# Two cross-attention layers on one core: the softmax factors of layer 0 applied by GpSimd to the exponentials, one step ahead of their turn

## The chip, the core and the metric

The kernel runs on one core of a Trainium2 chip. A core has five engines that run side by side, each with its own queue of instructions taken in order: TensorE (PE, matrix products), VectorE (DVE), ScalarE (ACT), GpSimd (POOL) and SyncE (SP), which here issues DMA transfers. They wait for each other by semaphores. TensorE writes to PSUM, eight banks of 128 x 512 fp32 values; SBUF holds everything else. The metric is device time in microseconds (us) for the whole program, from its start to its end; smaller is better. All data are fp32.

## What is computed

There are four batches of 1024 rows `x` (512 wide) and 1024 context rows (384 wide), and two attention layers one after the other. Cut to what matters:

```python
# layer 0: 16 heads of 64
h = layernorm(x, gamma, beta)
Q, K, V = (h @ Wq), (context @ Wk), (context @ Wv)        # by heads
attn = softmax(Q K^T, axis=-1) * 64 ** -0.5
x = x + (attn V) @ Wo + bo
# layer 1: 16 heads of 32
xn = x * rsqrt(mean(x * x) + eps) * norm_w
q, k, v = xn @ wq, split(context @ wkv)
q, k = normalized(rotated(q)), normalized(rotated(k))
x = x + (softmax(q k^T * sqrt(32)) v) @ wout
```

Note that the scale of layer 0 stands after the softmax: each row of exponentials is divided by its sum `l` and multiplied by 1/8.

## The kernel before

The work of a batch runs in two stages, layer 0 and then layer 1; the change concerns layer 0 and the passage from one to the other.

**Steps of layer 0.** Heads go in pairs: `NPAIR` = 8 pairs `p`, two heads `j` of 64 features each, side by side in the 128 partitions. For each pair there are `NT` = 8 steps `i`, one per tile of 128 query rows. So a batch has 64 steps and the program 256. One step (`Attention0.step`, L381) does this:

- `scores` (L367): four fp32 matrix products write the scores of 128 queries against 1024 keys for both heads into two PSUM tiles, `s`. There are just two such tiles, so the scores of the next step wait until the exponentials of this one have read theirs.
- For each head VectorE takes the negated maximum of a row (L395), and ScalarE writes the exponential to `e` in SBUF and its row sum to `l` (L396).
- VectorE turns `e` in 32 x 32 blocks (L401). Two steps (`BQ` = 2) make a block; after the odd step SP issues sixteen transfers of 128 KB each (L407) that put the 32 x 32 pieces where a whole transposition wants them, in `eT`.
- VectorE takes 1/l (L408).

**Products and factors.** A block of `eT` stands in the queue `self.blocks` until `product` (L443) multiplies it with the values `v`: 32 matmuls of 256 columns. Since `eT` has the keys in the partitions, the result `av` has features in the partitions and queries along the free axis, and the factors 1/l, which belong to queries, have to be spread along the features and transposed as well. `factors` (L418) lets GpSimd spread them, times 1/8, into `rb`; `factors_turned` (L431) has TensorE transpose `rb` into PSUM (`rT`, two 128 x 128 transposes, L440) and ScalarE copy it into `vals` (L441); the product ends with a VectorE multiply of `av` and these factors into `vals` (L456). All this is done in even steps, right after the scores, once two blocks are waiting: the block of steps 2 and 3 is multiplied in step 6.

**Filling.** All the other work of TensorE, the projections of later pairs, the output products `po` of earlier pairs and the first projections of layer 1, is cut into units with a cost in us. `Units.fill(us)` issues units until that cost is spent. The main loop (L798 to L809) divides what is left by the steps left, takes off the cost of a product (`AV` = 3.9) in steps that have one, and hands the rest to `step`. Before the change 1.8 us of a step's filling stand between the exponentials and the turns, the rest at the end. Filling units can bring VectorE additions (L301), ScalarE evacuations (L130), GpSimd work and DMA issues. The work of `rotate` (L494, the rotation of layer 1's q and k on all engines) can be put behind the turns by `post` and `flush`.

**Order on the queues.** Everything is issued by hand in program order; each engine takes its own instructions in that order. A transfer that waits on SP holds the loads and stores issued after it.

**Buffers.** `e` and `eT` (tag `big`) have two buffers each, `qk` (keys and queries of a pair, and of layer 1) four. PSUM banks `f0` to `f3` go round for all products but the scores.

**Change of layer** (L820 to L835). After the last step two blocks wait. Their products are put into the units: the first at once, the second after four output tiles, the statistics of layer 1's norm, and one projection.

## Time and profile before

| What | us |
|---|---|
| median of three runs | 2974.82 (2970.41 to 2974.82) |
| the profiled execution | 2969.33 |
| its span, first to last instruction | 2967.1 |
| one batch of layer 0, first scores of a batch to its last, batch 0 | 442 (25.5 to 467.3) |
| the four batches' stretches 60:480, 784:1214, 1518:1950, 2253:2685 together | 1714.0, of which PE 1699.0, DVE 1328.7, ACT 708.7, POOL 158.9 busy |
| pairs 6 and 7 of batch 0, 386:472 | 86.0, of which PE 84.8, DVE 76.1, POOL 19.4 busy |
| TensorE clock granted | 0.999 of full |

A row of the groups reads: line, engine, operation, tiles out<-in with shapes, xcount, then busy us in total and mean ns of one, then the idle time of the engine just before them and which work ended it. A row of the timeline reads: start and duration in us, engine, line, operation, tiles, how many were merged, and in brackets the idle time before and what ended it. "SPq" rows are the issuing of transfers, not the transfers themselves; a transfer lands later. A matmul's duration includes its way through the array, so two matmuls one after the other overlap, and what one costs is seen from start to start. The counted matmuls are twice those in the code where the array is split in two column halves.

Three more groups of the page that are not shown below: the factors' copy on ScalarE (L441) has 128 rows of 373 ns, VectorE's multiply with them (L456) 128 of 408 ns, its reciprocals (L408) 256 of 124 ns.

### The profile page before, as it was taken

How to read it: one execution, taken by the hardware profiler on the slowest of the kernel's cores; microseconds unless marked ns; L12 is line 12 of the kernel's file. 1: busy time of each engine (PE TensorE's matmuls, PEld its weight loads, DVE VectorE, ACT ScalarE, POOL GpSimd, SP SyncE). 2: the span in 40 equal slices, each digit the busy share in tenths (PEclk: the TensorE clock that was granted, in tenths of full speed). 3: DMA queues.
4: the chain of work that ended last, by engine and by line, in shares of the span. 5: the costliest groups of instructions: out<-in, count | busy, mean ns of one | idle time of the engine just before them, and what ended most of it. 6: DMA issues, size and time to landing. Idle time of an engine off the chain costs nothing.

```text
span 2967.1 us, 66793 instructions
## 1 busy us (share of the span) xinstructions
PE 2905.4 (98%) x27880; PEld 1454.7 (49%) x27880; DVE 2230.9 (75%) x2824; ACT 1430.4 (48%) x2265; POOL 417.2 (14%) x392
## 2 busy tenths in 40 slices
PE   8999999999999999999999999999999999999998
PEld 4544445555544444555544444455455444445544
DVE  4777795877777779587777777958767777785777
ACT  3444443666544444466644444446664443444664
POOL 0010022420000002232000000224100000023310
PEclk9999999999999999999999999999999999999999
DMA  5787674010388867301048777730105978772000
GB/s 146 173 198 181 158 178 111 21 35 25 80 205 192 186 159 179 91 22 35 25 100 214 182 182 171 165 79 22 35 25 120 211 177 186 166 171 62 2 2 30
DMA packets 177549, 348.88 MB, mean 118 GB/s; under 512 B 37600, under 2 KB 93152, under 8 KB 177248
## 3 DMA queue, kind: packets, MB, share of 16 engines
q1 hardware_dynamic: 175056, 343.43, 48.9%
q8 instruction: 220, 3.60, 0.5%
q10 hardware_dynamic: 2192, 1.19, 0.1%
q14 instruction: 81, 0.66, 0.1%
HBM read 67.64 MB, written 8.39 MB: 26 GB/s over the span
## 4 chain that ended last, share of the span: by engine, by line
PE 85%; DVE 7%; DMA 2%; ACT 2%; SPq 1%; issue 1%; POOL 1%; DVEq 0%; ACTq 0%
PE s L372 16%; PE av L449 14%; PE po L158 11%; PE pv L158 8%; PE s L597 7%; PE pqT L158 7%; PE av L636 6%; PE pkT L158 5%; PE q_p L158 3%; PE av L647 2%; PE k_p L158 2%; DVE both L613 2%; PE rT L440 1%; DVE both L617 1%; SPq L407 1%
## 5 line engine op out<-in xcount | busy, mean ns | idle before, releaser
L396 ACT ACTIVATE e<-s,m 128x1024 f32<-128x1024 f32 x512 | 566.1, 1110 | 666.3 <-DVE m L395 625.8
L395 DVE TENSOR_REDUCE m<-s 128x1 f32<-128x1024 f32 x512 | 602.7, 1219 | 314.0 <-PE s L372 314.0
L607 ACT ACTIVATE e<-s 128x1024 f32<-128x1024 f32 x512 | 496.7, 1022 | 312.4 <-PE s L597 297.3
L401 DVE STREAM_TRANSPOSE e<-e 128x1024 f32<-128x1024 f32 x512 | 606.7, 1223 | 47.6 <-ACT e L396 44.7
L372 PE MATMUL s<-qk 64*128 64x512 f32 x2048 | 521.3, 615 | 5.4 <-ACT e L396 4.7
L449 PE MATMUL av<-eT,v 128*64 128x256 f32 x4096 | 465.2, 380 | 7.3 <-DMA eT<-e 3.7
L613 DVE TENSOR_TENSOR both<-e 128x512 f32<-128x512 f32 x512 | 342.1, 700 | 125.0 <-ACT e L607 89.8
L449 PEld LDWEIGHTS av<-eT,v 128*64 128x64 f32 x4096 | 295.1, 137 | 186.2 <-issue 48.4
L372 PEld LDWEIGHTS s<-qk 64*128 64x128 f32 x2048 | 182.4, 186 | 269.2 <-issue 193.3
L597 PE MATMUL s<-q,k 32*128 32x256 f32 x4096 | 305.1, 401 | 5.8 <-ACT q L524 2.7
L597 PEld LDWEIGHTS s<-q,k 32*128 32x128 f32 x4096 | 191.2, 184 | 149.2 <-ACT e L607 72.0
L158 PE MATMUL po<-wo,vals 128*64 128x512 f32 x1024 | 239.7, 599 | 3.0 <-ACT v L130 3.0
L158 PE MATMUL pqT<-hT,w 128*64 128x512 f32 (+1 forms) x1216 | 241.4, 598 | 0.7 <-ACT hT L255 0.7
L441 ACT COPY vals<-rT 128x256 f32<-128x256 f32 x128 | 47.8, 373 | 323.7 <-PE rT L440 323.7
L301 DVE TENSOR_TENSOR x<-x,po 128x512 f32<-128x512 f32 x200 | 134.0, 678 | 83.0 <-PE po L158 82.7
L158 PEld LDWEIGHTS pv<-w,cT 128*64 128x64 f32 (+1 forms) x3648 | 168.5, 128 | 34.3 <-issue 31.2
L158 PE MATMUL pv<-w,cT 128*64 128x128 f32 (+1 forms) x3648 | 183.4, 274 | 0.0
L158 PE MATMUL pkT<-cT,w 128*64 128x512 f32 (+1 forms) x912 | 182.0, 601 | 0.9 <-ACT cT L130 0.9
L617 DVE TENSOR_TENSOR both<-both 128x1024 f32<-128x1024 f32 x128 | 159.7, 1248 | 4.4
L636 PE MATMUL av<-e,v 128*32 128x256 f32 x2048 | 137.1, 385 | 0.0
L636 PE MATMUL av<-e,rest 128*32 128x256 f32 x2048 | 137.0, 385 | 0.0
L158 PE MATMUL q_p<-wq,hT 128*32 128x256 f32 (+1 forms) x1920 | 131.2, 380 | 0.0
(461 smaller groups left out, 2482.0 us busy)
## 6 DMA issues: line engine op xcount, KB each, us to landing
eT<-e SPq DMA_DIRECT2D x2048, 128.0 KB, 2.4
xr<-in_x_dram SPq DMA_DIRECT2D x32, 256.0 KB, 4.1
x<-in_x_dram SPq DMA_DIRECT2D x32, 256.0 KB, 3.7
wo<-in_Wo_dram SPq DMA_DIRECT2D x16, 512.0 KB, 4.2
out_dram<-x SPq DMA_DIRECT2D x32, 256.0 KB, 2.6
w<-in_Wq_dram SPq DMA_DIRECT2D x31, 256.0 KB, 4.0
c<-in_ctx_dram SPq DMA_DIRECT2D x32, 192.0 KB, 3.8
wkv<-in_wkv_dram SPq DMA_DIRECT2D x16, 384.0 KB, 3.2
```

The costliest lines, as they stand in the source:

```text
L158: nc.tensor.matmul(o[rr], lhsT[:, rr], rhs, start=start, stop=stop)
L301: nc.vector.tensor_add(xt[t], xt[t], pp[0])
L372: nc.tensor.matmul(sc[j][:, kb * 512 : (kb + 1) * 512], pr["qT"][r[j], i * P : (i + 1) * P], pr["kT"][r[j], kb * 512 : (kb + 1) * 512], st ...
L395: nc.vector.tensor_reduce(m[:, j : j + 1], sc[j], AX.X, ALU.max, negate=True)
L396: nc.scalar.activation(e[j], sc[j].rearrange("p (g s) -> p g s", g=4), AF.Exp, bias=m[:, j : j + 1], accum_out=l[:, j : j + 1])
L401: nc.vector.transpose(e[j], e[j])
L449: nc.tensor.matmul(av[r[j], :W].rearrange("p (t a i) -> p t a i", t=BQ, a=4), pr["v"][:, k, r[j]], eT[:, j, :, :, k * 32 : (k + 1) * 32], ...
L597: nc.tensor.matmul(sc[j // 2][:, j % 2, c, :], kT[rr, g, k * P : (k + 1) * P], qT[rr, g, qb * WQ : (qb + 1) * WQ], start=True, stop=True,)
L607: nc.scalar.activation(e, sc[u], AF.Exp, scale=float(np.sqrt(np.float32(HD1))))
L613: nc.vector.tensor_add(self.both[:, kk, 2 * u : 2 * u + 2, :], es[u][:, :, 0, :], es[u][:, :, 1, :])
L617: nc.vector.tensor_add(self.both[:, 0], self.both[:, 0], self.both[:, kk])
L636: nc.tensor.matmul(self.av[rr, 0, :], v[g][:, 2 * kk + c, rr], es[j // 2][:, j % 2, c, :], start=first and c == 0, stop=end and c == 1,)
```

## The change

GpSimd multiplies each head's exponentials by 1/l and by 1/8, in place, before they are turned. VectorE turns them not in their own step but in the next one, between the two reciprocals of that step. In even steps the exponentials go to a tile of their own, `raw`, and the turn carries them into the block's tile `e`; in odd steps they go to `e` at once. The sixteen transfers of a block are issued in the following even step, after the turns. The product, now without factors, is evacuated by ScalarE (`evac`) and is issued in odd steps right after the exponentials' and turns' instructions, ahead of all filling, which now stands at the end of the step in one piece. The spread, transposed and copied factors are gone, and so are `post` and `flush`: `rotate` is issued where it arises.

`qk` has three buffers instead of four; the keys of layer 1 are allocated at pair 6 by a unit, its queries after layer 0, and the second half's queries lie in the buffer of `raw`. The output products of earlier pairs are added to the units at step 4 instead of 3. At the change of layer `end` turns the last step's exponentials and issues the last block's transfers; the two products then stand after four output tiles, the norm's statistics and a projection, and after the norm, its transposes and three more units' groups.

```diff
         def step(self, p, i, pr, us):
             n = f"{self.b}_{p}_{i}"
             sc = self.scores(p, i, pr)
-            if i % BQ == 0 and len(self.blocks) == 2:
-                self.factors_turned()
...
+            li = sb.tile([P, 2], F32, tag="li", bufs=3, name=f"li_{n}")
+            if i % BQ:
                 self.e = sb.tile([P, 4, BQ * 2, S // 4], F32, tag="e", bufs=2, name=f"e0_{n}")
-                self.li = sb.tile([P, BQ, 2], F32, tag="li", bufs=4, name=f"li_{n}")
-            e = [self.e[:, :, i % BQ * 2 + j, :] for j in range(2)]
+                e = [self.e[:, :, 2 + j, :] for j in range(2)]
+            else:
+                if self.raw is None:
+                    self.raw = sb.tile([P, 2, S], F32, tag="raw", bufs=1, name=f"raw_{self.b}")
+                e = [self.raw[:, j].rearrange("p (g s) -> p g s", g=4) for j in range(2)]
             for j in range(2):
                 nc.vector.tensor_reduce(m[:, j : j + 1], sc[j], AX.X, ALU.max, negate=True)
                 nc.scalar.activation(e[j], sc[j].rearrange("p (g s) -> p g s", g=4), AF.Exp, bias=m[:, j : j + 1], accum_out=l[:, j : j + 1])
-            holds["posts"] = True
-            self.u.fill(min(us, 1.8))
-            holds["posts"] = False
             for j in range(2):
-                nc.vector.transpose(e[j], e[j])
-            flush()
...
-            nc.vector.reciprocal(self.li[:, i % BQ, :], l)
...
+                if self.turn:
+                    self.turn[j]()
+                nc.vector.reciprocal(li[:, j : j + 1], l[:, j : j + 1])
+                nc.gpsimd.tensor_scalar(e[j], e[j], li[:, j : j + 1], HD0**-0.5, ALU.mult, ALU.mult)
+            if self.turn and i % BQ == 0:
+                self.regroup()
+            self.turn = [lambda j=j: nc.vector.transpose(self.e[:, :, i % BQ * 2 + j, :], e[j]) for j in range(2)]
+            self.now = p, i // BQ, pr
+            if i % BQ and len(self.blocks) == 2:
+                self.product()
+            self.u.fill(us)
+
+        def regroup(self):
+            p, q, pr = self.now
+            eT = sb.tile([P, 4, BQ * 2, S // 4], F32, tag="big", bufs=2, name=f"eT_{self.b}_{p}_{q}")
+            for g in range(4):
+                for k in range(4):
+                    nc.sync.dma_start(eT[32 * g : 32 * (g + 1), k], self.e[32 * k : 32 * (k + 1), g])
+            self.blocks.append((p, q, pr, eT.rearrange("p a (t h) s -> p h t a s", h=2)))
+
+        def end(self):
+            for f in self.turn:
+                f()
+            self.regroup()
...
-            nc.vector.tensor_mul(o, av[:, :W], o)
+            evac(pr["vals"][:, q * W : (q + 1) * W], av[:, :W])
...
-                if i == 3:
+                if i == 4:
...
-                now = 0.0 if i % 2 or len(att.blocks) < 2 else AV
+                now = AV if i % 2 and len(att.blocks) == 2 else 0.0
...
-                todo = work.total() + left + later + AV * (n // 2)
+                todo = work.total() + left + later + AV * ((n + 1) // 2)
...
+        att.end()
...
-        kT1, qT1 = qk_tile(f"k1_{b}_1"), qk_tile(f"q1_{b}_1")
+        begin("q")
+        kT, qT = kq["k"], kq["q"]
+        kT1, qT1 = qk_tile(f"k1_{b}_1"), sb.tile([P, 2, S], F32, tag="raw", bufs=1, name=f"q1_{b}_1")
...
-        att.factors_turned()
-        work.add([(AV, second)] + flat(outs[:4]) + norms[0]["stats"])
-        work.add(k1[0][0] + [(0.2, att.factors_turned)] + norms[0]["apply"] + [(AV, att.product)])
-        work.add(norms[0]["turn"] + q[0][0] + k1[1][0] + k1[0][2] + flat(outs[4:]) + q[0][2])
+        work.add(flat(outs[:4]) + norms[0]["stats"] + k1[0][0] + [(AV, att.product)] + norms[0]["apply"])
+        work.add(norms[0]["turn"] + q[0][0] + k1[1][0] + k1[0][2] + [(AV, att.product)] + flat(outs[4:]) + q[0][2])
```

`regroup` reads `self.now` of the step before: the block it issues ends with that step.

More of the change, by code (lines that the diff above doesn't have):

```diff
@@ L158, in matmul @@
             nc.tensor.matmul(o[rr], lhsT[:, rr], rhs, start=start, stop=stop)
-    posts = []
-    holds = {"posts": False}
-    def post(f):
-        if holds["posts"]:
-            posts.append(f)
-        else:
-            f()
-    def flush():
-        while posts:
-            posts.pop(0)()
     def rsqrt(o, v):
@@ L321, in project @@
             if what == "kT" and h == 0 and k == 0:
-                qk = sb.tile([P, 2, S], F32, tag="qk", bufs=4, name=f"qk0_{n}")
+                qk = sb.tile([P, 2, S], F32, tag="qk", bufs=3, name=f"qk0_{n}")
                 res["kT"], res["qT"] = qk[:, 0], qk[:, 1]
@@ L365, in __init__ @@
             self.blocks = deque()
+            self.turn = self.raw = None
         def scores(self, p, i, pr):
@@ L383, in step @@
             sc = self.scores(p, i, pr)
-            if i % BQ == 0 and len(self.blocks) == 2:
-                self.factors_turned()
             m = sb.tile([P, 2], F32, tag="m", bufs=3, name=f"m_{n}")
             l = sb.tile([P, 2], F32, tag="l", bufs=3, name=f"l_{n}")
-            if i % BQ == 0:
+            li = sb.tile([P, 2], F32, tag="li", bufs=3, name=f"li_{n}")
+            if i % BQ:
                 self.e = sb.tile([P, 4, BQ * 2, S // 4], F32, tag="e", bufs=2, name=f"e0_{n}")
-                self.li = sb.tile([P, BQ, 2], F32, tag="li", bufs=4, name=f"li_{n}")
-            e = [self.e[:, :, i % BQ * 2 + j, :] for j in range(2)]
+                e = [self.e[:, :, 2 + j, :] for j in range(2)]
[3 more added lines that the diff above has]
+                e = [self.raw[:, j].rearrange("p (g s) -> p g s", g=4) for j in range(2)]
             for j in range(2):
@@ L396, in step @@
                 nc.scalar.activation(e[j], sc[j].rearrange("p (g s) -> p g s", g=4), AF.Exp, bias=m[:, j : j + 1], accum_out=l[:, j : j + 1])
-            holds["posts"] = True
-            self.u.fill(min(us, 1.8))
-            holds["posts"] = False
             for j in range(2):
-                nc.vector.transpose(e[j], e[j])
-            flush()
-            if i % BQ == BQ - 1:
-                eT = sb.tile([P, 4, BQ * 2, S // 4], F32, tag="big", bufs=2, name=f"eT_{n}")
-                for g in range(4):
-                    for q in range(4):
-                        nc.sync.dma_start(eT[32 * g : 32 * (g + 1), q], self.e[32 * q : 32 * (q + 1), g])
@@ L408, in step @@
-            nc.vector.reciprocal(self.li[:, i % BQ, :], l)
-            if i % BQ == BQ - 1:
-                eT = eT.rearrange("p a (t h) s -> p h t a s", h=2)
-                self.blocks.append((p, i // BQ, pr, eT, self.li))
-            elif self.blocks:
-                if len(self.blocks) == 2:
-                    self.product()
-                self.factors()
-            self.u.fill(us - min(us, 1.8))
-        def factors(self):
-            li = self.blocks[0][4]
-            self.rb = sb.tile([P, BQ, P], F32, tag="rb", bufs=2, name=f"rb_{self.blocks[0][:2]}")
-            nc.gpsimd.tensor_scalar(
-                self.rb.rearrange("p t (j d) -> p (t j) d", j=2),
-                li.rearrange("p t j -> p (t j)").unsqueeze(2).to_broadcast([P, 2 * BQ, HD0]),
-                HD0**-0.5,
-                0.0,
-                ALU.mult,
-                ALU.add,
-            )
@@ L431, in factors_turned @@
-        def factors_turned(self):
-            p, q, pr = self.blocks[0][:3]
+                if self.turn:
[5 more added lines that the diff above has]
+            self.turn = [lambda j=j: nc.vector.transpose(self.e[:, :, i % BQ * 2 + j, :], e[j]) for j in range(2)]
@@ L434, in factors_turned, with product @@
+        def end(self):
+            for f in self.turn:
+                f()
+            self.regroup()
+        def product(self):
+            p, q, pr, eT = self.blocks.popleft()
             W = BQ * P
@@ L436, in factors_turned @@
                 pr["vals"] = sb.tile([P, S], F32, tag="vals", bufs=4, name=f"vals0_{self.b}_{p}")
-            self.o = pr["vals"][:, q * W : (q + 1) * W]
-            rT = bank(f"rT_{self.b}_{p}_{q}")
-            for k in range(BQ):
-                nc.tensor.transpose(rT[:, k * P : (k + 1) * P], self.rb[:, k, :], ident)
-            nc.scalar.copy(self.o, rT[:, :W])
-        def product(self):
-            p, q, pr, eT, _ = self.blocks.popleft()
-            o, W = self.o, BQ * P
             av = bank(f"av_{self.b}_{p}_{q}")
@@ L491, in project @@
             if i == TH - 1 and k == nk - 1:
-                post(lambda: rotate(t0, pp))
+                rotate(t0, pp)
         def rotate(t0, pp):
@@ L513, in turn_over @@
         def turn_over(t0):
-            flush()
             t1 = tiles.pop(t0)
@@ L523, in turn_over @@
                     )
-            nc.scalar.copy(dst[:, :, t0 * P : (t0 + TH) * P], pt.rearrange("p (g t) -> p g t", g=2))
+            nc.scalar.copy(dst()[:, :, t0 * P : (t0 + TH) * P], pt.rearrange("p (g t) -> p g t", g=2))
         return [
@@ L535, in qk_tile @@
     def qk_tile(name):
-        return sb.tile([P, 2, S], F32, tag="qk", bufs=4, name=name)
+        return sb.tile([P, 2, S], F32, tag="qk", bufs=3, name=name)
     class RowScratch:
@@ L775, in xattn_kernel, with begin @@
             if p == 6:
-                kT, qT = qk_tile(f"k1_{b}_0"), qk_tile(f"q1_{b}_0")
-                k = rotated_chains(kT, ct, NC_, lambda k, wk=wk: wk[:, k, :], f"k1_{b}_0", RowScratch())
-                other = k[0][0] + outs[0] + k[1][0] + outs[1] + k[0][2] + outs[2] + k[2][0] + k[1][2] + outs[3]
+                kq = {}
+                def begin(n, kq=kq, b=b):
+                    kq[n] = qk_tile(f"{n}1_{b}_0")
+                k = rotated_chains(lambda kq=kq: kq["k"], ct, NC_, lambda k, wk=wk: wk[:, k, :], f"k1_{b}_0", RowScratch())
+                other = [(0.0, lambda: begin("k"))] + k[0][0] + outs[0] + k[1][0] + outs[1] + k[0][2] + outs[2] + k[2][0] + k[1][2] + outs[3]
             if p == NPAIR - 1:
@@ L787, in xattn_kernel, with begin_v @@
                 v = []
-                def begin():
+                def begin_v():
                     v.extend(sb.tile([P, NT, P], F32, tag="v", bufs=3, name=f"v1_{b}_0_{g}") for g in range(2))
@@ L794, in xattn_kernel @@
                 reload = [(0.0, lambda wk1=wk1: wk1.append(half_kv_load(1, 0)))]
-                other = last[0] + k[3][0] + reload + last[1] + k[2][2] + last[2] + [(0.0, begin)] + vs[0][0]
+                other = last[0] + k[3][0] + reload + last[1] + k[2][2] + last[2] + [(0.0, begin_v)] + vs[0][0]
                 other += last[3] + vs[1][0] + k[3][2] + vs[2][0] + vs[3][0]
@@ L817, in xattn_kernel @@
             store_all()
+        att.end()
         tmp = Scratch(b)
         wv1, wq1 = half_kv_load(1, 1), half_q_load(1)
-        kT1, qT1 = qk_tile(f"k1_{b}_1"), qk_tile(f"q1_{b}_1")
-        q = rotated_chains(qT, xnT, NQ, lambda k, wq=wq: wq[0][:, k, :], f"q1_{b}_0", tmp)
-        k1 = rotated_chains(kT1, ct, NC_, lambda k, wk1=wk1: wk1[0][:, k, :], f"k1_{b}_1", tmp)
-        q1 = rotated_chains(qT1, xnT, NQ, lambda k: wq1[:, k, :], f"q1_{b}_1", tmp)
-        def second():
-            att.product()
-            att.factors()
-        att.factors_turned()
-        work.add([(AV, second)] + flat(outs[:4]) + norms[0]["stats"])
-        work.add(k1[0][0] + [(0.2, att.factors_turned)] + norms[0]["apply"] + [(AV, att.product)])
-        work.add(norms[0]["turn"] + q[0][0] + k1[1][0] + k1[0][2] + flat(outs[4:]) + q[0][2])
+        begin("q")
+        kT, qT = kq["k"], kq["q"]
+        kT1, qT1 = qk_tile(f"k1_{b}_1"), sb.tile([P, 2, S], F32, tag="raw", bufs=1, name=f"q1_{b}_1")
+        q = rotated_chains(lambda kq=kq: kq["q"], xnT, NQ, lambda k, wq=wq: wq[0][:, k, :], f"q1_{b}_0", tmp)
+        k1 = rotated_chains(lambda kT1=kT1: kT1, ct, NC_, lambda k, wk1=wk1: wk1[0][:, k, :], f"k1_{b}_1", tmp)
+        q1 = rotated_chains(lambda qT1=qT1: qT1, xnT, NQ, lambda k: wq1[:, k, :], f"q1_{b}_1", tmp)
+        work.add(flat(outs[:4]) + norms[0]["stats"] + k1[0][0] + [(AV, att.product)] + norms[0]["apply"])
+        work.add(norms[0]["turn"] + q[0][0] + k1[1][0] + k1[0][2] + [(AV, att.product)] + flat(outs[4:]) + q[0][2])
         work.drain()
```

## The prediction

> **What bounds the kernel now.** I read the page first: busy times, then the chain of waits, then the costliest groups.

> ```profile
> span 2967.1 us, 66793 instructions
> ...
> PE 2905.4 (98%) x27880; PEld 1454.7 (49%) x27880; DVE 2230.9 (75%) x2824; ACT 1430.4 (48%) x2265; POOL 417.2 (14%) x392
> ...
> PE 85%; DVE 7%; DMA 2%; ACT 2%; SPq 1%; issue 1%; POOL 1%; DVEq 0%; ACTq 0%
> ...
> L395 DVE TENSOR_REDUCE m<-s 128x1 f32<-128x1024 f32 x512 | 602.7, 1219 | 314.0 <-PE s L372 314.0
> ...
> L401 DVE STREAM_TRANSPOSE e<-e 128x1024 f32<-128x1024 f32 x512 | 606.7, 1223 | 47.6 <-ACT e L396 44.7
> ...
> L449 PE MATMUL av<-eT,v 128*64 128x256 f32 x4096 | 465.2, 380 | 7.3 <-DMA eT<-e 3.7
> ```

> TensorE is busy nearly throughout and holds 85% of the chain, while VectorE stands 314 us waiting for scores: TensorE's issue time is the bound, so what leaves its queue is worth its full issue time. POOL at 14% has room.

> Then the timeline of a stretch in the middle of layer 0 (start, duration, engine, line):

> ```profile
> 266.34 1.99 PE L372 MATMUL s<-qk 64*128 64x512 f32 x8
> ...
> 267.29 11.01 SPq L407 DMA_DIRECT2D eT<-e  x16
> 267.45 0.41 POOL L422 TENSOR_SCALAR rb_(4, 0)_2148<-li 128x256 f32<-128x256 f32 x1 [13.46 <-DVE li L408]
> ...
> 280.31 1.99 PE L372 MATMUL s<-qk 64*128 64x512 f32 x8
> ...
> 282.23 0.44 PE L440 MATMUL rT<-ident,rb_(4, 0)_2148 128*128 128x128 f32 x2
> 282.33 2.35 DVE L395 TENSOR_REDUCE m<-s 128x1 f32<-128x1024 f32 x2 [2.24 <-PE s L372]
> 282.59 1.08 PE L158 MATMUL pqT<-hT,w 128*64 128x512 f32 x4
> 282.70 0.37 ACT L441 COPY vals<-rT 128x256 f32<-128x256 f32 x1 [3.50 <-PE rT L440]
> ...
> 283.50 3.62 PE L449 MATMUL av<-eT,v 128*64 128x256 f32 x32
> ```

> Two things are to be seen. The two transposes of the factors hold PE's queue from 282.23 to 282.59, 0.36 us; so often, once a block. And the sixteen transfers of one block take SP 11.0 us of the 13.97 us that two steps last (266.34 to 280.31); the product at 283.50 reads their result. Transfers are the second bound, close behind.

> The tightest steps come early, by the same view:

> ```profile
> 107.15 2.17 PE L372 MATMUL s<-qk 64*128 64x512 f32 x8
> ...
> 108.66 10.57 SPq L407 DMA_DIRECT2D eT<-e  x16
> ...
> 119.58 2.17 PE L372 MATMUL s<-qk 64*128 64x512 f32 x8
> ...
> 122.96 3.62 PE L449 MATMUL av<-eT,v 128*64 128x256 f32 x32
> ```

> Two steps are 12.43 us here; issue ends at 119.23, the page gives 2.4 us from issue to landing, the product starts at 122.96: about 1.5 us spare.

> [...] the factors' broadcast, 256 elements, takes 0.41 us, against 0.25 us for 16 elements of L506 undisturbed, and two inputs of 512 (L290) 1.27 us.[...]

> **The change part by part.**

> *Factors through TensorE go.* 4 batches x 32 blocks = 128 times 0.36 to 0.37 us: -47 us, all on the path. With them go 128 GpSimd broadcasts (0.41 us) and 128 ScalarE copies (0.37 us), which lay beside PE.

> *Evacuation of the product.* VectorE's 128 multiplies of 0.41 us become 128 ScalarE copies of the size of L441, 0.37 us: ScalarE keeps its load (48% of the span), VectorE loses 52 us. The copy waits for the product; behind it are the projections' evacuations, and exponentials end about as the product does. Nothing. VectorE gets 256 reciprocals more, 0.12 us each: +31 us, thus -21 us net.

> *Multiplies on GpSimd.* 512 of 128x1024. From the slope between 16 and 256 elements (0.65 ns each) 0.9 us;[...] as if two-input (L290's slope, about 2.1 ns) 2.4 us. I take 1.1, ends 0.9 and 2.4. Nothing is not excluded below: it is added work, but the transposes need not wait for the current exponentials any more. Counted from the end of a step's scores: reductions until 2.4, turn until 3.7, reciprocal, first multiply from 3.9; second from 5.1. With 1.1 us they end at 6.2, with 2.4 at 8.7. Steps last 5.5 to 7.2 us, and the next step's turns begin 2.4 and 3.7 us after its scores, so at 7.9 and 9.2 at the earliest: hidden with either end. The cover is gone above about 3.3 us. The two rotations' POOL work in pairs 6 and 7 (0.25 + 2.93 + 1.05 us each) comes four times in sixteen steps and fits between.

> *Turns one step later.* A wait for exponentials (44.7 us of VectorE idle) goes; new waits are for POOL, above. Behind a turn are the reciprocal, the fill's additions, and the next reductions, which ScalarE and then the next scores wait for. In pairs 6 and 7 VectorE is near full (76.1 of 86 us in the window 386:472) and PE loses up to 2.06 us in waits for exponentials there. I book -5 us in all for these.

> *Transfers one step later, products one step later, and at the head of the step.* This is what could take the gain back. Before, the transfers begin 5.1 us after the scores of an odd step; the product comes three steps later after its scores, 0.37 us of factor transposes, and 0.9 to 1.8 us of fill. Now they begin about 5.0 us after the scores of an even step (both reductions and both turns), and the product comes three steps later straight after the scores. Typical: three steps = 1.5 x (13.97 - 0.37) = 20.4, less 5.0 leaves 15.4 against 11.0 + 2.4 = 13.4: 2 us spare. Tight: 1.5 x (12.43 - 0.37) - 5.0 = 13.1 against 10.6 + 2.4 = 13.0: nothing spare. Where loads of weights, rows and stores share the queue the sixteen issues take up to 12.4, once 15 us, and land up to 5 us later. Going through the blocks by the trace's SP and PE rows, with every block's own issue and step times, some 20 of 120 come short, together by 22 to 34 us. Before, such waits already lengthen product starts by some 10 us (2.1 us at most). I take +15 us, ends 0 and +45. SP passes the loads in another order: weight loads of a fill now stand behind the block's transfers, not in front; they have a pair's time (52 us) to land, so only their sharing of bandwidth counts, inside these ends.

> *Change of layer.* The last turn waits for POOL, transfers begin about 8.6 instead of 5.1 us after step 7's scores. Their product now stands behind about 22 us of PE work (eight output units, three projections, the other product, the norm), and they need 13. Nothing. The fewer query/key buffers are taken after their readers: pair 5 at pair 6, 6 and 7 only at the layer's end; the "raw" buffer is re-used over half a batch later. Nothing.

> Sum: -47 - 5 + 15 = -37 us. Against the profiled execution (span 2967.1, with what lies around it 2969.3) that is 2932; the median shown, 2974.8, is 5.5 us above that execution, so on its scale 2937.

> **Rivals.**
> - *Nearly all is given back to transfers.* The SP rows speak for it; against it 2 us spare in most blocks. At the upper end +45: 2974.8 - 47 + 45 = 2973 at most, in its middle near 2963.
> - *More is won*: later transfers never bind, and VectorE's lighter queue frees pairs 6 and 7: -47 - 10 = 2918.
> - *Slower: the product waits for transfers in every block.* The place is the odd step's head. The point is 0.38 us of new stall per block (47/124). If the new order made 5 + 13.4 into 5 + 16 us, three steps of 20 us would fall short by 1 us every block: +124 - 47, about 3050. For it: tight stretches without a margin; against it: SP has less to do per block than two steps last.
> - *Slower: GpSimd too slow.* Two multiplies take longer than a step, from 3.4 us each. At 4 us, 256 steps of 8.0 instead of 6.8 us: +300, near 3270. Against it: both bounds above.

> **How the numbers follow.** Forecast 0.66; given back 0.14; more won 0.08; slower by transfers 0.08; slower by GpSimd 0.04. The range holds the forecast, the second and most of the third: 2914 to 2967. About 0.2% (6 us) is what a measurement of this kernel can tell from no change. The rival that gives back lands within it about a quarter of the time: faster 0.84, same 0.04, slower 0.12.

> **What would show it.** No PE rows on rT; scores are followed at once by fill in even steps and by the product in odd ones; steps shorter by about 0.18 us on the mean; POOL multiplies near 1.1 us and VectorE's turns without waits on them; PE waits of "av" for the transfer, 10 us before, grown to about 25. Wrong if multiplies exceed 3 us, if turns wait for POOL, or if "av" waits pass 50 us.

## The result and the profile after

The changed kernel takes 2981.20 us (median of seven runs, 2976.96 to 2989.40), the kernel before, beside it, 2970.73 us (seven runs, 2966.13 to 2974.82). The ratio is 1.0034 [1.0024, 1.0045]: slower by a third of a per cent. The forecast was 2937 us; the measured time lies 44 us above it.

The page of the changed kernel, in the same parts as the prediction showed of before (span, busy times, shares of the chain, groups):

```profile
span 2981.0 us, 67205 instructions
...
PE 2893.5 (97%) x27624; PEld 1450.6 (49%) x27624; DVE 2184.6 (73%) x2952; ACT 1436.8 (48%) x2265; POOL 937.0 (31%) x776
...
PE 78%; DVE 8%; DMA 5%; SPq 3%; issue 2%; ACT 2%; POOL 1%; ACTq 0%; DVEq 0%
...
L361 PE MATMUL s<-qk 64*128 64x512 f32 x2048 | 538.3, 622 | 8.3 <-ACT raw L387 7.1
L392 POOL TENSOR_SCALAR raw<-raw,li 128x1024 f32<-128x1024 f32 x256 | 286.2, 1118 | 758.2 <-DVE li L391 749.8
...
L422 PE MATMUL av<-eT,v 128*64 128x256 f32 x4096 | 481.5, 389 | 22.8 <-DMA eT<-e 13.5
...
L395 DVE STREAM_TRANSPOSE e<-raw 128x1024 f32<-128x1024 f32 x256 | 310.1, 1229 | 3.0 <-DMA eT<-e 2.2
...
L159 PE MATMUL po<-wo,vals 128*64 128x512 f32 x1024 | 239.2, 598 | 9.5 <-DVE rot L474 9.5
```

Two rows of the page before answer to these and were not shown yet:

```profile
L372 PE MATMUL s<-qk 64*128 64x512 f32 x2048 | 521.3, 615 | 5.4 <-ACT e L396 4.7
...
L158 PE MATMUL po<-wo,vals 128*64 128x512 f32 x1024 | 239.7, 599 | 3.0 <-ACT v L130 3.0
```

The whole difference of the spans, 13.9 us, can be read off TensorE. It idled 61.7 us before (span less busy) and 87.5 now: +25.8, of which the products' waits are 15.5 (7.3 to 22.8), the output products' 6.5 (3.0 to 9.5), the scores' 2.9 (5.4 to 8.3). Its busy time fell by 11.9 us only, though 256 transposes worth 47 us left the queue. The rest is in two rows whose instruction counts did not change: scores are 17.0 us busier (521.3 to 538.3), products 16.3 us (465.2 to 481.5). The same matmuls take longer, because in places the granted TensorE clock is 0.50: a matmul of the scores then lasts 1054 ns instead of 589. The trace has such stretches of half clock for 62.1 us of the span in the changed kernel, 7.3 us in the kernel before; in both some 4 us of it lie at the very end of the program. At a granted clock of 0.50 they cost half their length at most: 27 us more than before ((62.1 - 7.3) / 2). The remaining 6 us or more are counted as busy in rows of scores that stretch at full clock. The kernel before has such rows too, of 3.08 us in pair 7; in all they are some 5 us longer now, in pairs 0 and 6.

Where this happens is seen when the time from the first scores of a group of pairs to the first of the next is summed over the four batches, in each kernel's profiled execution (us; the last batch's last piece ends with TensorE's last matmul; e3, f1, f4 and f6 are experiments told of below):

| Stretch | before | after | e3 | f1 | f4 | f6 |
|---|---|---|---|---|---|---|
| pairs 0 to 2 | 661.4 | 666.4 | 653.2 | 659.5 | 651.4 | 655.7 |
| pairs 3 to 5 | 652.2 | 635.4 | 635.4 | 638.4 | 634.7 | 632.9 |
| pairs 6 and 7, to the first scores of layer 1 | 585.2 | 607.3 | 604.6 | 581.3 | 585.3 | 573.6 |
| layer 1, and the start of the next batch | 1038.0 | 1041.8 | 1040.4 | 1042.4 | 1035.3 | 1036.9 |

Each column is a single execution; those of e3 and f4 are 4 to 5 us shorter than the medians of their kernels, so differences of a few us between columns say little.

Pairs 3 to 5 win 16.8 us, close to what 48 products, 0.37 us less each, should give (17.8). Pairs 0 to 2 lose 5.0 where 40 products should have won 14.8; products wait for transfers there, and one stretch of half clock in each batch goes with such a wait. Pairs 6 and 7 with the passage lose 22.1 where 40 products should have won 14.8: that is where most of the forecast was lost.

The timeline of TensorE in pair 7 of batch 1, changed kernel (start, duration, line, operation; in brackets idle time and releaser). The pair's step 0 begins at 1153.37:

```profile
1153.37 1.99 PE L361 MATMUL s<-qk 64*128 64x512 f32 x8
...
1160.06 1.99 PE L361 MATMUL s<-qk 64*128 64x512 f32 x8
1161.97 3.67 PE L422 MATMUL av<-eT,v 128*64 128x256 f32 x32
1165.78 3.08 PE L361 MATMUL s<-qk 64*128 64x512 f32 x8
1170.62 4.91 PE L361 MATMUL s<-qk 64*128 64x512 f32 x8 [1.77 <-ACT raw L387]
1175.46 4.96 PE L422 MATMUL av<-eT,v 128*64 128x256 f32 x32
1180.35 1.99 PE L361 MATMUL s<-qk 64*128 64x512 f32 x8
1182.27 1.94 PE L159 MATMUL po<-wo,vals 128*64 128x512 f32 x8
```

Steps 1 and 3 hold scores and a product and nothing else, step 2 scores alone. The kernel before, in the same place (its steps 1 to 3):

```profile
1156.06 1.99 PE L372 MATMUL s<-qk 64*128 64x512 f32 x8
1157.98 0.66 PE L519 MATMUL k_t<-ident,rot 128*128 128x128 f32 x4
1158.56 1.94 PE L158 MATMUL po<-wo,vals 128*64 128x512 f32 x8
1161.68 3.08 PE L372 MATMUL s<-qk 64*128 64x512 f32 x8 [1.18 <-ACT e L396]
1164.68 0.44 PE L440 MATMUL rT<-ident,rb_(6, 3)_9648 128*128 128x128 f32 x2
1165.05 3.67 PE L449 MATMUL av<-eT,v 128*64 128x256 f32 x32
1168.66 1.99 PE L372 MATMUL s<-qk 64*128 64x512 f32 x8
```

There step 1 has filling, step 2 a product, and no half clock follows the wait of 1.18 us. In the changed kernel, with 2 us of work in step 2, TensorE must wait for the exponentials (1.77 us before step 3, and once more inside the row of 4.91 us, for the second head). And the scores and product of step 3 take 4.91 and 4.96 us instead of 1.99 and 3.67. The windows of the same stretch, cut in pieces of 3.41 us, show the clock (window, then length and busy us of PE, PEld, DVE, ACT, POOL with counts, granted PE clock, DMA share, GB/s):

```profile
1164.47:1167.88 3.41, 3.28 (x19) 1.33 (x16) 3.41 (x5) 2.56 (x5) 3.24 (x3) 1.00 0.96 212
1167.88:1171.30 3.42, 1.65 (x6) 0.44 (x3) 3.32 (x5) 1.94 (x3) 1.61 (x2) 1.00 0.94 206
1171.30:1174.71 3.41, 3.41 (x8) 1.17 (x6) 2.32 (x5) 0.40 (x2) 2.23 (x2) 0.50 0.21 48
1174.71:1178.12 3.41, 3.41 (x15) 1.52 (x16) 2.94 (x5) 2.41 (x4) 0.04 (x1) 0.50 0.85 189
1178.12:1181.54 3.42, 3.42 (x28) 1.93 (x26) 1.05 (x2) 0.37 (x1) 2.20 (x2) 1.00 0.91 204
```

One piece in which PE is busy for 1.65 of 3.42 us is followed by two at clock 0.50, in which it has work throughout. The other three batches show the same 6.8 us in pair 7. The pair's outside units (output products and projections of layer 1) arrive at step 4; from there on the steps are full.

### The profile page after: what moved, and what is told of

Read it like the earlier page. It is cut to its first block, busy times and chain, and to the rows that moved or that the text cites. A ratio compares the mean times of both kernels' runs of the same rounds, so it can differ in the third digit from the quotient of the medians.

```text
span 2981.0 us, 67205 instructions
## 1 busy us (share of the span) xinstructions
PE 2893.5 (97%) x27624; PEld 1450.6 (49%) x27624; DVE 2184.6 (73%) x2952; ACT 1436.8 (48%) x2265; POOL 937.0 (31%) x776
## 4 chain that ended last, share of the span: by engine, by line
PE 78%; DVE 8%; DMA 5%; SPq 3%; issue 2%; ACT 2%; POOL 1%; ACTq 0%; DVEq 0%
PE s L361 15%; PE av L422 13%; PE po L159 10%; PE s L569 7%; PE pv L159 7%; PE av L608 6%; PE pqT L159 6%; PE pkT L159 4%; PE q_p L159 3%; DMA eT<-e 3%; SPq L406 3%; PE av L619 2%; PE k_p L159 2%; DVE both L585 2%; DVE m L386 1%
## 5 line engine op out<-in xcount | busy, mean ns | idle before, releaser
L386 DVE TENSOR_REDUCE m<-s 128x1 f32<-128x1024 f32 x512 | 603.4, 1220 | 430.2 <-PE s L361 429.5
L361 PE MATMUL s<-qk 64*128 64x512 f32 x2048 | 538.3, 622 | 8.3 <-ACT raw L387 7.1
L392 POOL TENSOR_SCALAR raw<-raw,li 128x1024 f32<-128x1024 f32 x256 | 286.2, 1118 | 758.2 <-DVE li L391 749.8
L387 ACT ACTIVATE e<-s,m 128x1024 f32<-128x1024 f32 x256 | 282.9, 1109 | 487.4 <-DVE m L386 311.6
L422 PE MATMUL av<-eT,v 128*64 128x256 f32 x4096 | 481.5, 389 | 22.8 <-DMA eT<-e 13.5
L387 ACT ACTIVATE raw<-s,m 128x1024 f32<-128x1024 f32 x256 | 285.2, 1114 | 437.7 <-DVE m L386 437.5
L392 POOL TENSOR_SCALAR e<-e,li 128x1024 f32<-128x1024 f32 x256 | 286.0, 1118 | 518.9 <-DVE li L391 255.1
L422 PEld LDWEIGHTS av<-eT,v 128*64 128x64 f32 x4096 | 296.7, 139 | 246.5 <-issue 106.8
L361 PEld LDWEIGHTS s<-qk 64*128 64x128 f32 x2048 | 190.2, 187 | 305.2 <-issue 161.9
L395 DVE STREAM_TRANSPOSE e<-raw 128x1024 f32<-128x1024 f32 x256 | 310.1, 1229 | 3.0 <-DMA eT<-e 2.2
L395 DVE STREAM_TRANSPOSE e<-e 128x1024 f32<-128x1024 f32 x256 | 310.1, 1230 | 0.2
L159 PEld LDWEIGHTS pv<-w,cT 128*64 128x64 f32 (+1 forms) x3648 | 170.7, 128 | 33.3 <-issue 27.9
```

The lines of the kernel that those rows point to most:

```text
L159: nc.tensor.matmul(o[rr], lhsT[:, rr], rhs, start=start, stop=stop)
L361: nc.tensor.matmul(sc[j][:, kb * 512 : (kb + 1) * 512], pr["qT"][r[j], i * P : (i + 1) * P], pr["kT"][r[j], kb * 512 : (kb + 1) * 512], st ...
L386: nc.vector.tensor_reduce(m[:, j : j + 1], sc[j], AX.X, ALU.max, negate=True)
L387: nc.scalar.activation(e[j], sc[j].rearrange("p (g s) -> p g s", g=4), AF.Exp, bias=m[:, j : j + 1], accum_out=l[:, j : j + 1])
L392: nc.gpsimd.tensor_scalar(e[j], e[j], li[:, j : j + 1], HD0**-0.5, ALU.mult, ALU.mult)
L395: self.turn = [lambda j=j: nc.vector.transpose(self.e[:, :, i % BQ * 2 + j, :], e[j]) for j in range(2)]
```

## The experiments

In each expectation the theories are named with what they say. Ratios are to the kernel before, run beside each. "Than after" compares ratios with 1.0034.

**The multiply left out.**

```diff
-                nc.gpsimd.tensor_scalar(e[j], e[j], li[:, j : j + 1], HD0**-0.5, ALU.mult, ALU.mult)
```

> The changed kernel without GpSimd's multiply: 1/l and 1/8 are left out of the result, the turns wait for the exponentials of the step before alone. Theory A (the multiplies of 1.12 us lie wholly beside other work): within 3 us of the changed kernel, ratio to before 1.002 to 1.005. Theory B (turns or transfers wait for GpSimd, or it slows VectorE): 10 us or more less than the changed kernel, ratio below 1.000.

2977.73 us, ratio 1.0021 [1.0013, 1.0028] (the result then lacks 1/l and 1/8): 0.13% or 4 us less than after, with intervals that overlap; this is within theory A's ratios, though a little over its 3 us. GpSimd's 572 us of multiplies are hidden almost wholly, and the wait of turns for GpSimd isn't the loss.

**Odd pairs and the first two get their units a step earlier.**

```diff
-                if i == 4:
+                if i == (3 if p % 2 or p < 2 else 4):
```

> The changed kernel with one condition altered: the outside work of a pair is added to the units at step 4 only in even pairs from 2 on (whose output products need the last product of the pair before) and at step 3 in all others. Theory A (TensorE runs out of filling units in steps 1 to 3 of pair 7, so these steps have scores and products alone, last only as long as the exponentials take, and the granted clock falls): pair 7 from its step 4 to step 7 falls from 27.9 to about 23 us per batch, no slice near 0.66 of the clock in pair 7, whole program 15 to 25 us less than the changed kernel, ratio to before 0.995 to 0.998. Theory B (pair 7 is long because GpSimd or VectorE is late there): pair 7 as long as in the changed kernel, ratio to before 1.002 to 1.005.

2987.32 us, 1.0058 [1.0046, 1.0070]: slower still, above the ranges of both theories. The trace shows why the edit does not mend pair 7: at 1165.20 to 1185.65 of batch 1 there are again a step with only scores and a product, one with scores alone (1.77 us wait) and one at half clock, for units that come at step 3 come after step 2, the one that is empty. So it is not the move from step 3 to step 4 by itself that empties pair 7. In the kernel before, where units also came at step 3, products stood in even steps; step 2 had one, and the steps of pair 7 shown above have no step without either.

**A part of the filling between scores and product, as before.**

```diff
             if i % BQ and len(self.blocks) == 2:
+                self.u.fill(min(us, 1.8))
                 self.product()
-            self.u.fill(us)
+                self.u.fill(us - min(us, 1.8))
+            else:
+                self.u.fill(us)
```

> The changed kernel with up to 1.8 us of the step's filling issued before the product, as before the change. Theory A (at the head of an odd step the product stands in front of all filling and waits for its transfers, 44 us in all by the trace): part of those waits is covered by about 1 us of filling in odd steps; waits at product starts fall from 44 to about 25 us, pairs 0 to 2 shorter by 1 to 2 us per batch, program 5 to 15 us less than the changed kernel, ratio 0.998 to 1.002. Theory B (pairs 0 to 2 are held by SP's and the transfers' rate, so a product waits later for the same thing): program within 3 us of the changed kernel.

2970.77 us, 1.0001 [0.9992, 1.0009]: 10 us less than after. The page's row for the products:

```profile
L425 PE MATMUL av<-eT,v 128*64 128x256 f32 x4096 | 470.8, 383 | 10.6 <-DMA eT<-e 6.4
```

Idle 10.6 instead of 22.8 us, and 10.7 us less busy; in the table pairs 0 to 2 win 13.2 us, and none of the four stretches of half clock there is left (the granted clock of the profiled execution is 0.994 instead of 0.990). So the product at the head of the step did wait for transfers, and filling ahead of it covers about half of that. (The page has 22.8 us of idle time before products in the changed kernel; the 44 us of the expectation is another count, which no view here shows.)

**No weight loads between the transfers.** The weights of the first pair of a batch are used for all its pairs, in after (e4) and in before (e4b).

```diff
-                    w[p + 1] = pair_load(b, p + 1)
+                    w[p + 1] = w[p]
```

> The changed kernel without the loads of the weights of pairs 1 to 7: all pairs of a batch use those of pair 0, so the result is another; 84 loads of 192 to 256 KB fall away from SP's queue, all else stays. Theory A (transfers sharing SP and the engines with loads hold pairs 0 to 2): waits at product starts in pairs 1 to 5 fall by half or more, pairs 1 and 2 last about 1 to 1.5 us less each than in the changed kernel, program 10 to 20 us less, ratio 0.997 to 1.000. Theory B (something else holds these pairs): pairs 0 to 2 unchanged.

> The kernel before without the loads of the weights of pairs 1 to 7 (all pairs use those of pair 0, so the result is another). Theory A (the order of before covers most of what loads do to transfers): 2 to 8 us less than before, ratio 0.997 to 1.000, against 10 us for the changed kernel. Theory B (loads cost both orders alike): 10 us or more less, ratio below 0.9965.

2971.91 us, 0.9996 [0.9987, 1.0006] for the changed kernel: 0.38% or 11 us less than after. 2962.75 us, 0.9973 [0.9964, 0.9981] for the kernel before: 8 us less. The first is in theory A's range; the second is at the edge of theory A's and short of theory B's. For the whole program the loads cost both orders nearly the same: the difference is about 3 us, and the intervals don't separate it from none, nor from twice as much. In the profiled executions pairs 0 to 2 win 17.1 us without loads in the changed kernel and 8.8 in the kernel before, so in these pairs loads may weigh more in the new order; single executions don't settle that.

**Pair 7 gets its units from its first step.**

```diff
-                if i == 4:
+                if i == (0 if p == NPAIR - 1 else 4):
```

> The changed kernel with pair 7's outside work (output products of pairs 4 and 5, projections of layer 1) added to the units at its step 0 instead of 4; pairs 0 to 6 as in the changed kernel. Theory A (steps 1 to 3 of pair 7 have no filling, TensorE is idle enough there for the clock to be halved for 6.8 us per batch): no half clock in pair 7, pair 7 and the passage to layer 1 together from 178.3 to about 173 us per batch, program 15 to 25 us less than the changed kernel, ratio 0.995 to 0.999. Theory B (pair 7 has more work than it had and no stretch without filling counts): pair 7 and passage as in the changed kernel, ratio 1.002 to 1.005.

2954.45 us, 0.9940 [0.9928, 0.9953]: 28 us less than after, from one line, and more than the 15 to 25 of theory A. The same steps of pair 7, in this kernel:

```profile
1149.39 1.99 PE L361 MATMUL s<-qk 64*128 64x512 f32 x8
1151.31 3.67 PE L422 MATMUL av<-eT,v 128*64 128x256 f32 x32
1154.81 1.03 PE L159 MATMUL po<-wo,vals 128*64 128x512 f32 x4
1155.77 1.99 PE L361 MATMUL s<-qk 64*128 64x512 f32 x8
1157.68 2.81 PE L159 MATMUL k_p<-wkv,cT 128*64 128x256 f32 x24
...
1163.74 1.99 PE L361 MATMUL s<-qk 64*128 64x512 f32 x8
1165.65 3.67 PE L422 MATMUL av<-eT,v 128*64 128x256 f32 x32
```

Step 2 (1155.77) is now full, the waits for exponentials are gone (the scores' idle time on the page is 0.7 us instead of 8.3), the granted clock in pair 7 of batch 1 is 1.00, and scores take 521.8 instead of 538.3 us. In the table pairs 6 and 7 with the passage win 26.0 us. The products' idle time is unchanged, 23.0 us: this loss is another than e3's.

How much of the 28 us is clock can be estimated. Half clock falls from 62.1 to 28.1 us of the span (granted clock 0.990 and 0.995 in the two profiled executions), worth 17 us at most ((62.1 - 28.1) / 2). The granted clock of all runs says less: 0.990 or 0.991 in each run of the changed kernel, 0.993 to 0.995 here, a loss of about 28 and 17 us, so some 12 us of difference. The rest is waiting.

**Both.** f4 has the edits of f1 and e3.

> The changed kernel with both edits: up to 1.8 us of filling ahead of the product in odd steps, and pair 7's outside work from its step 0. Theory A (two separate losses, at product heads and in pair 7): the two gains add, -10 from the first and -15 to -25 from the second against the changed kernel, ratio 0.992 to 0.996. Theory B: no more than the better of the two alone.

2944.23 us, 0.9903 [0.9886, 0.9919]: 1.3% or 39 us less than after, where the two apart give 28 and 10. They add, as theory A has it; the sum is past its range because pair 7's part is larger than was expected.

**The kernel before without factors.** Factors, transposes and the multiply after the product are left out, ScalarE evacuates; all else stays in the old order (the result lacks 1/l and 1/8).

```diff
-            if i % BQ == 0 and len(self.blocks) == 2:
-                self.factors_turned()
...
-                self.factors()
...
-            nc.vector.tensor_mul(o, av[:, :W], o)
+            evac(o, av[:, :W])
```

> The kernel before with the factors left out: no spread on GpSimd, no two transposes, no copy; the product is evacuated by ScalarE; the result lacks 1/l and 1/8. The order of all else is that of before. Theory A (the removal is worth 0.37 us a block when the order of before is kept, and the loss comes from the new order): ratio 0.982 to 0.987, -38 to -52 us. Theory B (transfers take the removal back in any order): ratio 0.992 to 0.999.

2938.76 us, 0.9886 [0.9871, 0.9901]: 34 us less than before (38.9 in its profile, the fastest of its four runs by 8.7 us), not 47; the ratio lies between the two theories. Pairs 3 to 5 take 631.3 us, 20.9 less than before; pairs 6 and 7 with the passage 578.0, 7.2 less, where 14.8 were to be had. So even under the old order part of the removal is lost there: pair 7 waits for exponentials 1.21 us in each batch, as before the change.

Against this kernel the changed one is 44 us slower by the ratios (1.0034 less 0.9886): that is what the new order and the multiply cost together, and the multiply has some 4 us of it.

**Layer 1's first keys earlier.** In f4, two key projections of pair 6 are added at step 2 instead of 4.

```diff
+                early = [(0.0, lambda: begin("k"))] + k[0][0] + k[1][0]
...
+                if p == 6 and i == 2:
+                    work.add(early)
```

> The changed kernel with pair 7's outside work from step 0, filling ahead of the product, and in pair 6 the first two key projections of layer 1 from step 2, the rest from step 4. Theory A (pair 6 also runs short of filling in steps 2 and 3 and then waits at a PSUM bank that the rotation still reads, 2.4 us per batch): pair 6 from 53.6 to about 52 us per batch, 5 to 10 us less than the kernel without this edit, ratio 0.989 to 0.994. Theory B (no loss in pair 6 but the bank's, which comes wherever the rotation falls): within 3 us of the kernel without this edit.

2961.16 us, 0.9960 [0.9947, 0.9972]: 17 us worse than f4, where theory A had 5 to 10 us less and theory B a difference of 3 us at most: both fell. From pair 7's first step in its timeline:

```profile
1149.22 1.94 PE L159 MATMUL po<-wo,vals 128*64 128x512 f32 x8
1153.85 2.93 PE L159 MATMUL po<-wo,vals 128*64 128x512 f32 x8 [2.70 <-DVE rot L477]
```

An output product waits 2.70 us for VectorE's rotation, not for exponentials or a transfer. It needs a PSUM bank. The changed kernel has the same in pair 6:

```profile
1130.48 0.60 PE L159 MATMUL k_p<-wkv,cT 128*64 128x256 f32 x4
...
1132.93 3.67 PE L422 MATMUL av<-eT,v 128*64 128x256 f32 x32
...
1140.70 1.89 PE L159 MATMUL po<-wo,vals 128*64 128x512 f32 x8
1142.52 0.66 PE L491 MATMUL k_t<-ident,rot 128*128 128x128 f32 x4
1145.55 1.94 PE L159 MATMUL po<-wo,vals 128*64 128x512 f32 x8 [2.38 <-DVE rot L474]
```

Four banks go round. The key projection `k_p` begun at 1130.48 takes one, the product `av` the next, an output the third, the transposition `k_t` the fourth, and the output after it the first again, which the rotation still reads; and the rotation stands on VectorE behind reductions and turns. In each batch this wait is 2.38 us, 9.5 us in all. The kernel before doesn't have it, nor does f5, which keeps the old order: it came with the new one.

**More TensorE work between a key projection and its bank's next user.** f6 is f4 with the units of pairs 6 and 7 in another order.

```diff
-... k[0][0] + outs[0] + k[1][0] + outs[1] + k[0][2] + outs[2] + k[2][0] + k[1][2] + outs[3]
+... k[0][0] + outs[0] + outs[1] + k[1][0] + k[0][2] + outs[2] + outs[3] + k[1][2] + k[2][0]
...
-                other = last[0] + k[3][0] + reload + last[1] + k[2][2] + last[2] + [(0.0, begin_v)] + vs[0][0]
+                other = last[0] + k[3][0] + reload + last[1] + last[2] + k[2][2] + [(0.0, begin_v)] + vs[0][0]
```

> The kernel with the split filling and pair 7's work from its start, and with the units of pairs 6 and 7 in another order: two output tiles stand together, so that the PSUM bank of a key projection is taken again after two output tiles and a transposition or projection (about 4 us of TensorE work) instead of after one tile and a transposition (2.3 us). Theory A (output products wait 2.45 and 1.57 us per batch for the bank that the rotation, standing behind VectorE's turns, still reads): both waits go, pairs 6 and 7 lose 8 instead of 24 us in all, 8 to 16 us less than without this edit, ratio 0.985 to 0.989. Theory B (the waits move to other instructions): within 4 us of the kernel without this edit, ratio 0.989 to 0.992.

2930.25 us, 0.9861 [0.9836, 0.9885]: 0.42% or 12 us less than f4 by the ratios, as theory A has it, and 40 less than before by the medians. Of all kernels here it is the fastest. With f1's 28 and e3's 10 the three edits give back more than the 44 us that the new order cost. Its page:

```profile
span 2929.3 us, 67187 instructions
...
PE 2863.4 (98%) x27624; PEld 1432.4 (49%) x27624; DVE 2184.0 (75%) x2952; ACT 1434.4 (49%) x2265; POOL 936.8 (32%) x776
...
L361 PE MATMUL s<-qk 64*128 64x512 f32 x2048 | 520.9, 615 | 0.7 <-ACT qk L131 0.7
...
L425 PE MATMUL av<-eT,v 128*64 128x256 f32 x4096 | 466.9, 381 | 10.9 <-DMA eT<-e 9.4
...
L159 PE MATMUL po<-wo,vals 128*64 128x512 f32 x1024 | 240.1, 599 | 4.3 <-DVE x L289 4.3
```

The rotation is gone as a releaser of output products (f4 had 15.0 us of it). TensorE is 42.0 us less busy than before and idles 65.9 us, 4.2 more: the removal, with the waits that the change added taken out again.

## Why the prediction was wrong

*Factors gone, -47.* Right as a price. Where least else binds, in pairs 3 to 5, 16.8 of 17.8 us came. Over the whole kernel the 47 came only as far as the places told of below allowed.

*Evacuation on ScalarE, nothing; VectorE lighter.* Held. ScalarE's copies of `av` take 372 ns. On VectorE the multiplies' 52.2 us went and the reciprocals' 31.7 us became 63.1, as said; summed one by one its instructions take 18.0 us less (2376.4 to 2358.4), near the 21 of that sum. The page's busy time fell by 46.3, because it counts the time in which two records overlap once.

*Multiply 1.1 us, hidden.* Right: 1118 ns, and leaving it out gives 4 us or less. It lies between the prediction's ends, above the 0.9 us that the slope between two instructions of the kernel before gives; the 1.1 itself was the author's estimate, which no trace of before showed. (The cover of 3.3 us holds for a step of 6.8 us; for the shortest steps named, 5.5 us, the same sum gives 2.65.) VectorE's turns took 1229 instead of 1223 ns and reductions 1220 as against 1219 beside more than twice the GpSimd work (937.0 instead of 417.2 us); that GpSimd leaves them at this pace was an assumption of the prediction, which no trace of before showed.

*Turns, -5 in pairs 6 and 7.* Failed. VectorE's wait for exponentials before a turn did go: of 44.7 us none is left, and all its idle time before turns is 3.2. But TensorE's waits for exponentials rose from 4.7 to 7.1 us, all in pair 7, because TensorE had too little to do there. Where the units arrive in time (f1) the scores' idle time is 0.7 us; the -5 was there to be had. (The 2.06 us that the prediction read here is idle time of the weight loads; the matmuls waited up to 1.18.)

*Transfers, +15.* The size in idle time was right: products waited 15.5 us more, of the 15 foretold. The trace puts 13.5 of the 22.8 us down to the blocks' own transfers and the rest mostly to loads between them; one wait alone is 4.6 us. (Of the tight step the prediction names 1.5 us spare; its lines give 1.3.) Not in the sum was the half clock after such waits, up to 6.8 us for the four stretches in pairs 0 to 2. Pairs 0 to 2 come out 19.8 us worse than the removal alone; e3 wins 13.2 of it back. The rival in which every block waits had the wrong mechanism: products wait 18 times in all, in pairs 1, 2 and 4 alone.

*Change of layer, nothing.* This is the step that failed. It looked at buffers and at the last two products, and gave no price to the rest of the same edit: products go to odd steps while pairs get their outside units at step 4. The prediction took for granted that each step has filling ("scores are followed at once by fill in even steps"). In pair 7, the last of its batch, no later projection is left to take from, so steps 1 to 3 ran dry. Of the 36.9 us that pairs 6 and 7 with the passage fall short of the removal, f1's line gives back 26.0; f6's order of banks with e3's split another 7.7 (581.3 to 573.6); 3.2 stay, which is within what single executions differ by. Also without a price was that `rotate` is issued where it arises, among reductions and turns: outputs wait 9.5 us for its PSUM bank in pair 6.

The forecast of 37 us less was reached in size by f6 (37.8 less in the profiles), not by the kernel it was made for. The gain there is the removal, but that the sums agree is partly luck: TensorE is 42.0 us less busy, not 47, and products wait 3.6 us more than before (7.3 to 10.9), not 15. "Slower" had a chance of 0.12, and neither of the two mechanisms that carried it is what happened.

What stays open: the clock was not varied by an edit alone. f1 fills the steps and keeps the clock at once, so its 28 us are split into wait and half clock only by the estimate above. That half clock costs about its half length is supported by runs of one and the same kernel: over the 20 runs of e2, whose granted clock goes from 0.989 to 0.994, 1 us of lost clock (one less the clock, times the time) goes with 0.99 us of time, at a correlation of 0.79. Layer 1, which the change leaves alone, is 3.8 us longer; it has four stretches of half clock of 3.4 us where before has one, which fits but wasn't tested. What the last 3.2 us in pairs 6 and 7 are, and the third of the loss in pairs 0 to 2 that e3 leaves (6.6 of 19.8 us), was not tried.

## What to carry to other kernels

When an edit moves where work is added or where a fixed piece stands in a step, list for each step, the last round above all, what the busiest engine still has to do: a step that runs dry can cost more than was removed around it (f1's one line was worth 26 us in pairs 6 and 7, where 14.8 were to be won). Put something that is ready ahead of an instruction that waits for a transfer (e3: 10 us less than after). And when buffers go round, count who takes the same one again and whether its reader, queued behind other work, is done by then (f6: 12 us less than f4).

## What was not expected of the hardware

```profile
2014.40:2017.81 3.41, 1.75 (x20) 1.31 (x16) 3.34 (x7) 2.31 (x4) 0.00 (x0) 1.00 0.00 0
2017.81:2021.22 3.41, 3.41 (x53) 1.94 (x52) 3.38 (x5) 2.95 (x4) 2.65 (x2) 1.00 0.01 5
```

1.75 of 3.41 us were enough here; 1.65 of 3.42 in pair 7 were not. So in pair 7 a wait of 1.77 us was followed by 6.8 us at half clock, worth up to 3.4 us more. Not every wait is: the kernel before waits 1.18 us for exponentials in pair 7 of all four batches, a third of a window, and its granted clock stays at 1.00 there.
